# Group norms that run beside selective scans: statistics and application on ScalarE instead of VectorE

## The chip, the core and the metric

The kernel runs on one core of one Trainium2 chip. A core has a matrix engine (TensorE, PE in the profile), a vector engine (VectorE, DVE), an activation engine (ScalarE, ACT), a general engine (GpSimd, POOL) and a sync engine (SyncE, SP) that here only issues DMAs. Each engine works through its own queue in order, and the queues wait for each other through semaphores. The metric is the device time of one execution in microseconds (us), as the median of several runs.

## The reference

The input is four images of 96 channels and 64 x 64 pixels (L = 4096), in fp32. Four layers follow, each of the form x + layer(group_norm(x)):

```python
def _gn(v, G=32, eps=1e-5):          # 32 groups of 3 channels
    g = v.reshape(B_, G, C_ // G, H_, W_)
    m = jnp.mean(g, axis=(2, 3, 4), keepdims=True)
    s = jnp.var(g, axis=(2, 3, 4), keepdims=True)
    return ((g - m) / jnp.sqrt(s + eps)).reshape(v.shape)

x = x + layer0(_gn(x))    # attention to pooled positions, 5x5 depthwise convolution
x = x + layer1(_gn(x))    # four-direction selective scan, then a convolution block with a channel gate
x = x + layer2(_gn(x))    # one dense 3x3 convolution
x = x + layer3(_gn(x))    # 1x1 and depthwise convolutions, a second selective scan, a gated tail
```

A selective scan is a linear recurrence along the pixels, in four directions, for 192 channels with 16 states each: h = h * exp(delta * A) + (delta * u) * B, and y is the sum over the states of h * C.

So there are 16 group norms in all, four for each image. Each takes the mean and the variance over three channels and all pixels, subtracts the one and divides by the root of the other.

## The kernel before

**Two kinds of work side by side.** The main function is `streams`. Its scans are one long chain of *units*: eight scans (two layers times four images, in the order `SCANS`) of 384 units, 3072 units in all. A unit treats 8 channels x 16 states = 128 partitions and a chunk of 1024 pixels; twelve units make a *group* (96 channels, one chunk, one direction). All other layers are written as Python generators, `first`, `second` and `third`, one call per image, and are laid *beside* the scans by `BESIDE`: `first` of images 1, 2, 3 beside scans 0, 3, 4; `second` of the four images beside scans 1, 2, 5, 6; three `third` beside scan 7. `first(0)` runs alone ahead of the scans and `third(3)` alone after them; while they do, `solo[0]` is true.

- `first`: load x, group norm, attention (layer 0), group norm, and the input projection and depthwise convolution of layer 1 (`in_conv`).
- `second`: the rest of layer 1, group norm, the dense 3x3 convolution (layer 2), group norm, and layer 3 up to its `in_conv`, which stores the scan's input u (`u_row`, `u_col`) in DRAM.
- `third`: the rest of layer 3.

**One unit**, `unit(i)`, puts these into the engines' queues in this order: `fetch(i+4)` (SP: a DMA of 512 KB into the tile `rep`, one of ten buffers), then the first side step, `decays(i+2)` (ACT: an exponential in place on `rep`, L1815), `scan(i)` (DVE: the recurrence, L1836), `carry_on(i-1)` (ACT: one column copied, L1844), `times_c(i)` (POOL: product with C, L1848), on every third unit `collect` (PE: sum over states into `acc`), `drive(i+2)` (PE: into a PSUM tile `bx` of two buffers), perhaps a second side step, and `times_b(i+1)` (DVE: product with B, L1829). `prepare` makes the inputs of a later group in small steps, among them a logarithm (L1757), casts (L1774, L1777) and loads of u; DMAs queued by `later` go out one to three units afterwards. On every twelfth unit `output` adds `acc` to the result on DVE or copies it on ACT.

The order in each queue is this order of emission (`tc.manual_schedule()`); nothing is moved afterwards.

**How side work is portioned.** A generator yields a number for the price of the step just emitted, a tuple `(1,)` for one convolution tap, or nothing (`None`) after a matrix product, whose consumer is then emitted at the end of the unit. `Slots` runs it, on a budget that each unit tops up:

```python
owed = min(owed, 0.5) + PACE - (2.1 if i % 3 == 1 else 0.0)   # PACE = 3.5
```

Per unit there is one side step, and a second if more than 0.9 of the budget is left; in the units in which `prepare` has its first steps these take the first place. Eighteen units before the end of a scan (`LEAD` = 6), when the next scan's first group is prepared, its u must have been written. So one unit earlier, at unit 365 of 384, whatever the side work has left is emitted at once:

```python
if at == per - NG - LEAD - 1:
    work.run()
```

**The group norm before** (`group_norm`): eight `bn_stats` on slices of 512 pixels (L1043), `bn_aggr` (L1047), a product with the matrix `group` that averages over three channels (PE), a copy, a difference and a fused multiply-add on one column (DVE, L1053, L1055, L1057: the variance between the channels is added), a second product with `group`, the root on ACT (L1062), its reciprocal on DVE (L1064), and the application to four slices of 1024 pixels (DVE, L1066), in place (`xn`, the second norm's `X`) or into a padded image (`pad`). Its yields are 1, 1, 1, 1, 0.5, none, 0.5, none, 0.5, 1, 1, 1, 1.

**PSUM.** `bank()` gives one of two buffers of the tag `one` beside scans, in turn, to side work and to `prepare`; all matrix products go through the helper `mm` (L948), so that every one of them shows as this line and is told apart by its tiles.

Of the kernel before, what the change touches and what calls it, by code (L numbers as in the profile page):

```python
# [9 lines left out]
F32 = mybir.dt.float32  # L10
BF16 = mybir.dt.bfloat16
AF = mybir.ActivationFunctionType
ALU = mybir.AluOpType
AX = mybir.AxisListType
# [4 lines left out]
L = H * W  # L19
# [8 lines left out]
CH = 1024  # L28
NCH = L // CH
PCH = 512  # L30
# [162 lines left out]
def _view(t, slot, rows=None):  # L193
    n, m, shape = slot
    v = t[: rows or t.shape[0], n : n + m]
    if len(shape) == 1:
        return v
    names = "abcd"[: len(shape)]
    return v.rearrange(f"p ({' '.join(names)}) -> p {' '.join(names)}",
                       **{k: s for k, s in zip(names, shape)})  # L200
# [693 lines left out]
def streams(ctx: ExitStack, tc: tile.TileContext, x, wts, cst, out, wat, cat, flag):  # L894
# [3 lines left out]
    nc = tc.nc  # L898
    keep = ctx.enter_context(tc.tile_pool(name="keep", bufs=1))
    small = ctx.enter_context(tc.tile_pool(name="small", bufs=2))  # L900
# [17 lines left out]
    def cv(name):  # L918
        n, m, shape = cat[name]
        return _view(ct, (n if n < n0 else n - n1 + n0, m, shape))  # L920
# [11 lines left out]
    ident, group = cv("ident"), cv("group")  # L932
# [3 lines left out]
    eps, one, minus = (cols[:, j : j + 1] for j in range(3))  # L936
# [7 lines left out]
    def img(t):  # L944
        return t.rearrange("p (a b) -> p a b", b=W)

    def mm(o, lhsT, rhs, first=True, last=True):
        nc.tensor.matmul(o, lhsT=lhsT, rhs=rhs, start=first, stop=last)  # L948

    solo = [True]  # L950
    spare = []

    def bank():
        if solo[0]:
            if not spare:
                t = ps.tile([128, CH], F32, tag="bx", name="bx")
                spare.extend((t[:, PCH:], t[:, :PCH]))
            return spare.pop()
        return ps.tile([128, PCH], F32, tag="one", name="one")
# [47 lines left out]
    with tc.tile_pool(name="start", bufs=1) as T:  # L1007
# [9 lines left out]
        for tag in ("l1_", "l3_"):  # L1017
            decay[tag] = keep.tile([128, 4, E // 8], F32, name=tag + "decay")
            n, m, shape = cat[tag + "alogn"]
            src = _view(t0, (n - n2, m, shape))  # L1020
            if tag == "l3_":
                nc.scalar.activation(decay[tag], src, AF.Exp)
                src = decay[tag]
# [14 lines left out]

    def group_norm(src, dst):

        st = small.tile([96, 8, 6], F32, name="gn_st")
        for j in range(8):
            nc.vector.bn_stats(st[:, j, :], src[:, bass.ts(j, PCH)])  # L1043
            if j % 2:
                yield 1
        mv = small.tile([96, 2], F32, name="gn_mv")
        nc.vector.bn_aggr(mv, st.rearrange("p a b -> p (a b)"))  # L1047
        yield 0.5
        p1 = bank()
        mm(p1[:96, 0:1], group[:96], mv[:, 0:1])  # L1050
        yield
        g = small.tile([96, 2], F32, name="gn_g")
        nc.vector.tensor_copy(g[:, 0:1], p1[:96, 0:1])  # L1053
        d = small.tile([96, 1], F32, name="gn_d")
        nc.vector.tensor_sub(d, mv[:, 0:1], p1[:96, 0:1])  # L1055
        v = small.tile([96, 1], F32, name="gn_v")
        nc.vector.scalar_tensor_tensor(out=v, in0=d, scalar=d, in1=mv[:, 1:2], op0=ALU.mult, op1=ALU.add)  # L1057
        yield 0.5
        p2 = bank()
        mm(p2[:96, 0:1], group[:96], v)  # L1060
        yield
        nc.scalar.activation(g[:, 1:2], p2[:96, 0:1], AF.Sqrt, bias=eps[:96])  # L1062
        yield 0.5
        nc.vector.reciprocal(g[:, 1:2], g[:, 1:2])  # L1064
        for j in range(4):
            nc.vector.tensor_scalar(dst[:, 16 * j : 16 * j + 16, :], img(src)[:, 16 * j : 16 * j + 16, :],  # L1066
                                    g[:, 0:1], g[:, 1:2], ALU.subtract, ALU.mult)
            yield 1

    def diagonals(pool, w, name="diag"):  # L1070
# [229 lines left out]
    def first(b):  # L1300

        with tc.tile_pool(name="p1", bufs=1) as P:
            xn = P.tile([96, L], F32, name="xn")
            for j in range(4):
                nc.sync.dma_start(out=xn[:, bass.ts(j, CH)], in_=x[b][:, bass.ts(j, CH)])
            yield from group_norm(xn, img(xn))
            with tc.tile_pool(name="p1d", bufs=1) as D:
                samp = D.tile([96, 34, 34], F32, name="samp")
# [13 lines left out]
                with tc.tile_pool(name="p1f", bufs=1) as FP:  # L1322
                    feat = FP.tile([96, L], F32, name="feat")
                    yield from neighbours(b, xn, samp, dist, feat)
                    with tc.tile_pool(name="l0c", bufs=1) as pool:
# [12 lines left out]
                        for j in range(8):  # L1338
# [11 lines left out]
                            nc.sync.dma_start(out=res1[b][:, js], in_=xn[:, js])  # L1350
                            yield 1
            yield from group_norm(xn, img(xn))
            for j in range(4):
                nc.sync.dma_start(out=gate1[b][:, bass.ts(j, CH)], in_=xn[:, bass.ts(j, CH)])
# [20 lines left out]
    def second(b):  # L1375
# [90 lines left out]
        with tc.tile_pool(name="p2r", bufs=1) as R2:  # L1466
            hp = R2.tile([96, PADW, PADW], F32, name="hp")
            border(hp, 1)
            with tc.tile_pool(name="p2b", bufs=2) as pool:
                X = pool.tile([96, L], F32, name="X", bufs=1)  # L1470
                for j in range(4):
                    nc.sync.dma_start(out=X[:, bass.ts(j, CH)], in_=res1[b][:, bass.ts(j, CH)])
                pad = pool.tile([96, PADW, PADW], F32, name="pad2", bufs=1)
                border(pad, 1)
                w = staged(pool, "l2_k", "l3_c1", "l3_lin")
                yield from group_norm(X, pad[:, 1 : 1 + H, 1 : 1 + W])
                for j in range(8):
                    js = bass.ts(j, PCH)
                    p = bank()
                    yield from conv(p[:96], w["l2_k"], pad, j)  # L1480
                    nc.vector.tensor_add(X[:, js], X[:, js], p[:96])
                    nc.sync.dma_start(out=res2[b][:, js], in_=X[:, js])
                    yield 1

                yield from group_norm(X, img(X))
                for j in range(8):
                    js = bass.ts(j, PCH)
                    p = bank()
                    mm(p[:96], w["l3_c1"], X[:, js])
                    yield  # L1490
                    r = pool.tile([96, PCH], F32, name="r")
                    nc.scalar.activation(r, p[:96], AF.Relu, bias=bn3[1], scale=bn3[0])
                    yield 1
                    q = bank()
                    mm(q[:96], w["l3_lin"], r)
                    yield
                    nc.scalar.activation(inner(hp, j), img(q[:96]), AF.Identity, bias=wv("l3_lin_b"))
                    yield 1
# [481 lines left out]
    with tc.manual_schedule():  # L1980
# [15 lines left out]
        for i in range(total):  # L1996
            s, at = divmod(i, per)
# [29 lines left out]
    p = bank()  # L2027
# [36 lines left out]
```

## Time and profile before

| | us |
|---|---|
| median of three runs | 15068.81 (15060.3 to 15096.54) |
| the profiled execution, its own time | 15038.64 |
| its span, first to last instruction | 15036.8 |
| DVE busy | 11679.2 |
| PE busy | 12260.5 |
| POOL busy | 10375.2 |
| ACT busy | 8280.8 |
| scans on DVE, L1836 (3072, two groups) | 5401.4 + 1754.2 |
| products with B on DVE, L1829 (3072) | 3720.1 |
| products with C on POOL, L1848 (3072) | 7230.5 |
| scan factors on ACT, L1815 (3072) | 3495.9 |

The scans run from 830 us to about 14750 us of the span; each of the first seven takes 1689 to 1721 us and the eighth 1969. Busy times are unions of an engine's instructions. The mean granted clock of the matrix engine is 0.809 of full speed. A group of instructions in the profile is written as line, engine, operation, tiles written and read, shapes and count, then its busy time in us, the mean length of one in ns, and the idle time of the engine just before it, with what ended that. A line can be that of a helper. The profile's chain of work that ended last goes back only to the very end of this kernel, so stretches of time are read instead.

### The profile page before, as it was taken

The numbers are of one execution on the slowest core, as the hardware profiler recorded it, in microseconds if no ns is written. First come the engines' busy times: TensorE is split into PE (matmuls) and PEld (weight loads), VectorE is DVE, ScalarE is ACT, GpSimd is POOL, SyncE is SP. The second block draws the span as 40 slices with busy tenths as digits, with TensorE's granted clock in tenths as the row PEclk, the third lists the DMA queues.
The fourth block names the chain that finished last, engine by engine and source line by source line (L and its number), as shares of the span: only waits on it lengthen the run. The fifth ranks groups of instructions, "written<-read, shape, count | busy, mean of one in ns | idle before, by whom it ended". The sixth has DMA issues, their size and how long they took to land. (4 is left out here: it accounts for less than half of the span.)

```text
span 15036.8 us, 127166 instructions
## 1 busy us (share of the span) xinstructions
PE 12260.5 (82%) x40658; PEld 3344.2 (22%) x40658; DVE 11679.2 (78%) x7517; ACT 8280.8 (55%) x11648; POOL 10375.2 (69%) x4746
## 2 busy tenths in 40 slices
PE   8978886888969787889868887897969888667757
PEld 2322221222212222222212221221212222111111
DVE  0067888888878888778887798798878888777784
ACT  3155555555745566555655556455755567545652
POOL 0056787777868777668776787786777778666672
PEclk9978886898969888789867797797879888667666
DMA  0066788786878778667876788687877868666682
GB/s 9 26 149 163 177 202 213 175 211 171 215 178 203 195 183 209 167 168 197 208 179 158 170 204 222 174 203 180 203 195 192 203 173 221 168 166 167 167 204 68
DMA packets 902136, 2644.32 MB, mean 176 GB/s; under 512 B 107280, under 2 KB 257392, under 8 KB 901456
## 3 DMA queue, kind: packets, MB, share of 16 engines
q1 hardware_dynamic: 900800, 2634.83, 71.0%
q8 instruction: 323, 5.29, 0.2%
q14 instruction: 357, 2.92, 0.1%
q10 hardware_dynamic: 656, 1.27, 0.0%
HBM read 2169.08 MB, written 466.62 MB: 175 GB/s over the span
## 5 line engine op out<-in xcount | busy, mean ns | idle before, releaser
L1848 POOL TENSOR_TENSOR rep<-hs,bc 128x1024 f32<-128x1024 f32 x3072 | 7230.5, 2358 | 3160.0 <-DVE hs L1836 2682.5
L1836 DVE TENSOR_TENSOR_SCAN hs<-rep,carry,bx 128x1024 f32<-128x1024 f32 x2304 | 5401.4, 2344 | 277.9 <-POOL rep L1848 15.0
L1829 DVE TENSOR_TENSOR bx<-bx,bc 128x1024 f32<-128x1024 f32 x3072 | 3720.1, 1211 | 1033.6 <-PE bx L948 998.6
L1815 ACT ACTIVATE rep<-rep,l_decay 128x1024 f32<-128x1024 f32 x3072 | 3495.9, 1143 | 903.6 <-DMA rep<-dd 883.7
L948 PE MATMUL bx<-parts,spread 24*128 24x512 bf16 x6144 | 1413.5, 438 | 1812.0 <-DVE hs L1836 1762.5
L948 PE MATMUL acc<-rep,ct 128*32 128x512 f32 x12288 | 2603.0, 732 | 184.9 <-POOL rep L1848 184.9
L1836 DVE TENSOR_TENSOR_SCAN hs<-rep,bx 128x1024 f32<-128x1024 f32 x768 | 1754.2, 2284 | 306.9 <-POOL rep L1848 224.9
L948 PEld LDWEIGHTS <-spread 24*128 24x128 bf16 x6144 | 310.1, 93 | 4297.8 <-DVE hs L1836 2925.5
L948 PE MATMUL one<-band,dg 96*96 96x512 f32 x2304 | 1117.9, 621 | 0.0
L948 PE MATMUL one<-upad,diag 96*96 96x512 f32 x2016 | 1021.0, 643 | 3.2 <-ACT ur L1114 2.7
L948 PEld LDWEIGHTS acc<-rep,ct 128*32 128x32 f32 x12288 | 507.5, 126 | 1958.9 <-issue 1482.0
L948 PE MATMUL one<-qq,kk 96*128 96x512 f32 x1152 | 820.7, 802 | 133.8 <-ACT ex L1234 80.1
L1234 ACT ACTIVATE ex<-one 128x512 f32<-128x512 f32 x576 | 342.8, 595 | 754.1 <-PE one L948 749.3
L948 PE MATMUL one<-pr,ct 6*96 6x512 f32 x1024 | 647.1, 732 | 29.7 <-ACT pr L1720 4.1
L1815 ACT ACT_TABLE_LOAD x470 | 603.0, 1283 | 116.4 <-DMA rep<-dd 108.7
L948 PE MATMUL one<-hp,diag 96*96 96x512 f32 x1152 | 606.5, 665 | 48.0 <-POOL diag L1075 48.0
L948 PE MATMUL one<-vpad,diag 96*96 96x512 f32 x1200 | 590.7, 627 | 0.0
L1844 ACT COPY carry<-hs 128x1 f32<-128x1 f32 x2304 | 408.8, 177 | 314.4 <-DVE hs L1836 313.5
L948 PE MATMUL held<-ex,cols 128*32 128x256 f32 x3072 | 569.2, 451 | 12.0 <-ACT ex L1234 6.0
L948 PE MATMUL held<-ex,vT 128*32 128x256 f32 x3072 | 569.4, 451 | 0.0
L948 PEld LDWEIGHTS one<-band,dg 96*96 96x96 f32 x2304 | 350.6, 166 | 532.7 <-issue 517.1
L948 PEld LDWEIGHTS one<-upad,diag 96*96 96x96 f32 x2016 | 317.6, 172 | 490.0 <-issue 472.6
(3399 smaller groups left out, 13980.7 us busy)
## 6 DMA issues: line engine op xcount, KB each, us to landing
rep<-dd SPq DMA_DIRECT2D x3072, 512.0 KB
parts<-du SPq DMA_DIRECT2D x1024, 144.0 KB
bc<-rows SPq DMA_DIRECT2D x256, 512.0 KB
dd<-delta SPq DMA_DIRECT2D x256, 384.0 KB
du<-cut SPq DMA_DIRECT2D x256, 384.0 KB
us<-urow SPq DMA_DIRECT2D x128, 384.0 KB
du<-cut SPq DMA_DIRECT2D x256, 192.0 KB
yrow<-yo SPq DMA_DIRECT2D x128, 384.0 KB
```

The source lines that it names most:

```text
L948: nc.tensor.matmul(o, lhsT=lhsT, rhs=rhs, start=first, stop=last)
L1234: nc.scalar.activation(last.rearrange("p a b -> p (a b)"), p, AF.Exp, scale=HD**-0.5)
L1815: nc.scalar.activation(a, a, AF.Exp, scale=decay[tag][:, k, NG * h + m : NG * h + m + 1])
L1829: nc.vector.tensor_mul(bx, bx, ready[i // NG][2][:, 0, :])
L1836: nc.vector.tensor_tensor_scan(out=hs, data0=a, data1=bx, initial=carry[:, h, m : m + 1] if c else 0.0, op0=ALU.mult, op1=ALU.add)
L1844: nc.scalar.copy(carry[:, h, m : m + 1], live[i][1][:, CH - 1 : CH])
L1848: nc.gpsimd.tensor_tensor(a, hs, ready[i // NG][2][:, 1, :], ALU.mult)
```

## The change

Beside scans (`solo[0]` false) a new function takes the place of the old body; in the solo stages nothing is changed. The mean is taken from copies in place on ACT whose accumulator output gives the sum of a slice, the variance from squares of the difference on ACT (the result of the square goes into a PSUM bank that nobody reads; its accumulator output is what counts), and the application is an ACT operation with a scale and a bias per channel. DVE keeps two small reduces, the reciprocal and one product of two columns. The mean over the group is now taken before the squares, so the two passes over the image follow each other, and the new function yields 1 four times, 0.5, none, 0.5, 1 eight times, 0.5, none, 0.5, 0.5 and 1 four times.

```diff
--- before.py
+++ after.py
@@ -1038,6 +1038,9 @@
 
     def group_norm(src, dst):
 
+        if not solo[0]:
+            yield from group_norm_on_scalar(src, dst)
+            return
         st = small.tile([96, 8, 6], F32, name="gn_st")
         for j in range(8):
             nc.vector.bn_stats(st[:, j, :], src[:, bass.ts(j, PCH)])
@@ -1065,6 +1068,40 @@
         for j in range(4):
             nc.vector.tensor_scalar(dst[:, 16 * j : 16 * j + 16, :], img(src)[:, 16 * j : 16 * j + 16, :],
                                     g[:, 0:1], g[:, 1:2], ALU.subtract, ALU.mult)
+            yield 1
+
+    def group_norm_on_scalar(src, dst):
+
+        st = small.tile([96, 8], F32, name="gs_st")
+        for j in range(4):
+            s = src[:, bass.ts(j, CH)]
+            nc.scalar.activation(s, s, AF.Copy, accum_out=st[:, j : j + 1])
+            yield 1
+        mv = small.tile([96, 4], F32, name="gs_mv")
+        nc.vector.tensor_reduce(mv[:, 0:1], st[:, 0:4], AX.X, ALU.add)
+        yield 0.5
+        p = bank()
+        mm(p[:96, 0:1], group[:96], mv[:, 0:1])
+        yield
+        nc.scalar.activation(mv[:, 1:2], p[:96, 0:1], AF.Copy, scale=-1.0 / L)
+        yield 0.5
+        for j in range(8):
+            p = bank()
+            nc.scalar.activation(p[:96], src[:, bass.ts(j, PCH)], AF.Square, bias=mv[:, 1:2], accum_out=st[:, j : j + 1])
+            yield 1
+        nc.vector.tensor_reduce(mv[:, 2:3], st, AX.X, ALU.add)
+        yield 0.5
+        p = bank()
+        mm(p[:96, 0:1], group[:96], mv[:, 2:3])
+        yield
+        nc.scalar.activation(mv[:, 2:3], p[:96, 0:1], AF.Sqrt, bias=eps[:96], scale=1.0 / L)
+        yield 0.5
+        nc.vector.reciprocal(mv[:, 2:3], mv[:, 2:3])
+        nc.vector.tensor_mul(mv[:, 3:4], mv[:, 1:2], mv[:, 2:3])
+        yield 0.5
+        for j in range(4):
+            nc.scalar.activation(dst[:, 16 * j : 16 * j + 16, :], img(src)[:, 16 * j : 16 * j + 16, :], AF.Identity,
+                                 scale=mv[:, 2:3], bias=mv[:, 3:4])
             yield 1
 
     def diagonals(pool, w, name="diag"):
```

## The prediction

> **What bounds the kernel now.** I read the busy times of the page first. No engine is full over the span, so the answer has to come from stretches.
>
> ```profile
> PE 12260.5 (82%) x40658; PEld 3344.2 (22%) x40658; DVE 11679.2 (78%) x7517; ACT 8280.8 (55%) x11648; POOL 10375.2 (69%) x4746
> ```
>
> Next, the busy time of each engine in chosen stretches. Columns: stretch, length, busy us (instructions) of PE, PEld, DVE, ACT, POOL, then clock, DMA share, GB/s. The first three are group norms (seven scan units each: the second norm of `first`, both norms of `second`), the fourth has no side work (36 units), the fifth is the tail of `second`, depthwise convolutions (20 units).
>
> ```profile
> 2072.00:2106.00 34.00, 15.99 (x54) 3.50 (x54) 33.47 (x27) 15.14 (x18) 22.74 (x10) 0.60 0.86 225
> 3363.00:3399.00 36.00, 12.02 (x44) 2.79 (x44) 35.69 (x31) 10.54 (x11) 24.67 (x11) 0.57 0.78 194
> 3522.00:3558.00 36.00, 12.58 (x43) 3.04 (x44) 35.80 (x30) 12.60 (x18) 26.89 (x12) 0.53 0.79 198
> 2399.00:2540.00 141.00, 70.28 (x238) 12.41 (x236) 128.08 (x76) 71.25 (x92) 115.78 (x51) 0.58 0.88 214
> 4075.00:4157.00 82.00, 78.18 (x239) 23.09 (x238) 71.73 (x43) 63.77 (x78) 64.94 (x29) 0.92 0.80 198
> ```
>
> In a norm DVE is busy 98 to 99% and ACT a third to under half: DVE alone sets the pace, 4.9 to 5.2 us a unit. Without side work a unit takes 141/36 = 3.92 us, 3.56 of it DVE and 1.98 ACT. In the tail PE is 95% busy, 4.10 us a unit. Then the groups of DVE around a norm (3355 to 3400 us), where the third figure is idle time before the group:
>
> ```profile
> L1066 DVE TENSOR_SCALAR pad<-X,gn_g 96x1024 f32<-96x1024 f32 x4 | 5.3, 1330 | 0.0
> L1043 DVE BATCH_NORM_STATS2 gn_st<-X 96x6 f32<-96x512 f32 x8 | 5.1, 675 | 8.8 <-DMA X<-res 8.8
> L1057 DVE SCALAR_TENSOR_TENSOR gn_v<-gn_d,gn_mv 96x1 f32<-96x1 f32 x1 | 1.8, 1778 | 0.0
> ```
>
> The statistics also made DVE wait 8.8 us for the image. `gn_v` is one column wide yet takes 1.8 to 3.2 us beside scans and 0.22 in the solo stage.
>
> **What the Trainium skill says.** "SBUF — State Buffer", Who interferes with whom: DVE's two-port operations, and those with two SBUF inputs, exclude GpSimd from a shared port pair for a whole instruction; ACT waits for no one there. The trace agrees: `gn_v` above has two SBUF inputs and waits out a GpSimd product of 2.36 us. "ScalarE: Activation LUTs", What ACT_TABLE_LOAD costs: each per-partition pointer operand adds about 93 ns. The trace agrees: two pointers 776 ns (L1413), one 682 (L1434).
>
> **Removed from DVE**, per norm: 8 x 0.675 statistics = 5.4; aggregate 0.34; copy, difference and reciprocal 0.42; `gn_v` 2.5 (mean of the 14 beside scans); application 4 x 1.27 = 5.1 (mean over xn, X and pad). Sum 13.8 us, 14 norms: 193 us. The two solo norms are untouched.
>
> **Added to DVE**: two reduces of 0.15 and 0.16 (nearest rows, L1209 and L1440), reciprocal 0.14, and a product of two SBUF columns. No such product lies beside scans; bounds 0.14 (no GpSimd in the way) and 3.2 (worst `gn_v`); I take 2.5, its twin. Sum 2.95 a norm, 41 us. DVE loses 152 us net.
>
> **Added to ACT.** Prices from these rows of its groups (whole span, and for L1755 the tail):
>
> ```profile
> L1462 ACT ACTIVATE one<-V,se 96x512 f32<-96x512 f32 x32 | 21.3, 674 | 0.0
> L1434 ACT ACTIVATION_READ_ACCUMULATOR V<-one,wt 96x1 f32 x32 | 6.1, 189 | 0.0
> L1755 ACT ACTIVATE delta<-w__18893,cols 96x1024 f32<-96x1024 f32 x1 | 1.1, 1145 | 0.0
> L1062 ACT ACT_TABLE_LOAD x16 | 20.5, 1283 | 0.3
> ```
>
> Four in-place copies, 1.04 (L1774) + 0.19 = 1.23 each, 4.9. Eight squares into PSUM with a pointer, 0.67 + 0.19, 6.9. Four applications with two pointers, 1.145 + 0.09, 4.9. Two one-column operations, 0.5. Sum 17.3, of which 0.26 (the root) was there. Copy, Square and Identity have no table loads at their present lines (L1462, L1141, L1753), so the root's load and the reload after it, 2.6 us, stay as they are. ACT gains 17 x 14 = 239 us.
>
> **The planner.** A unit gives side work at most two steps, for a budget of 2.8 on average. The old norm is 11 steps, the new one 21 (a step that stops at a bare `yield` swallows the next 0.5); walked through `unit` and `Slots`, a norm takes 14 units in place of 7. So each scan with two norms needs 14 units more. In `first` the side work ends at unit 339 of 384 and would end at 353: idle units pay. In `second` it ends at unit 365 now, just where `work.run()` empties what is left (two steps). After, 35 steps are left: 31 convolution taps in one lump ahead of unit 365, in scans 1, 2, 5 and 6.
>
> **Price of the lump.** Two lines, of PE's timeline and of the waits from 4157 to 4238 us:
>
> ```profile
> 4148.92 3.67 PE L948 MATMUL one<-upad,diag 96*96 96x512 f32 x8
> PE one L948 <- DMA us<-urow: 13.9, 1, 13.9
> ```
>
> An fp32 tap leaves two records, so 62 x 0.46 = 28.5 us on PE. Behind it stand `drive(367)` on PE and `decays(367)` on ACT, the latter after the last Silu 0.68, transposing copy 1.10, table load 1.28 and exponential 1.14: 4.2. DVE meanwhile has scan 365, product 366, scan 366 and product 367, about 7.1. Stall 25.6. SP's queue stands too: the stores of u come before `fetch(369)` and before the next scan's load of u. That load already stops PE for 13.9 us here in `second` (one unit of 17.2); much of it moves into the lump: the load lands about 44 us after the lump starts and releases scan 369 at 47, where it would otherwise stand at 40; so 7 us of stall there, against 13.6 now. Net 25.6 - 6.6 = 19; I take 18 and keep 8 to 28.
>
> **The wait at the start.** The DVE waits ahead of the first statistics sum to 54 us in seven norms. Now ACT's copy waits. Behind it in ACT's queue is `decays(i+2)`, so DVE can still do two units. In-place copies also wait for the stores of res1 and res2 that read the image, which before only the application did; the last is issued a few units earlier and should have landed. I take 25 of the 54 as saved and keep 0 to 45.
>
> **The pace of a new norm.** From below DVE's own work, 3.56 + 2.95/14 = 3.77 a unit. ACT's busy time is 1.98 + (17.3 + 2.6)/14 = 3.40, so busy time alone doesn't bind. But ACT runs in order, waits 0.29 a unit for scan factors (883.7 us over 3072 units), and now has two waits per norm for a PE product, not one (5.6 us each when it waited); DVE's reduces and reciprocal wait for it. With 11 more per 14 units ACT would need 4.5. Its head start of two units hides most. I take 4.05, the no-side pace plus most of DVE's 0.21, range 3.9 to 4.2.
>
> **The sum.** The 14 norm windows last 522 us; three of them hold the pooling of `first` (5.9 each), so 504 for 98 units. The 98 further units that the new norms take displace 42 without side work (165 us) and 56 of the tail (230). Before: 899. After: 196 x 4.05 = 794, + 4 x 18 - 25 = 841. Gain 58 us of the profiled execution's 15038.6 (span 15036.8). The median shown, 15068.8, is 30 above it, with the same work; I put the gain on the median: 15010.
>
> **Rivals.** *ACT becomes the bound, slower.* If its waits add rather than hide, a norm unit takes 4.6: 902 + 72 - 0 - 899 = +75, so 15144. The point of decision is 4.22 with no start saved (4.35 with 25). For it: ACT is a single queue with 84% busy; against it: it is two units ahead and its peaks (two squares, a logarithm, two table loads) are about 4 us over three units. *The lump eats the gain.* With 30 a lump and 15 saved, 794 + 120 - 15 - 899 = 0: 15069. For it: the stall is worked out from queues, and stores follow it; against: the 13.9 us wait there overlaps. *ACT hides all.* 3.85 a unit, 10 a lump, 40 saved: 755 + 40 - 40 - 899 = -144: 14925. For it: half of ACT is idle in these windows. That the change does nothing is excluded: all norms beside scans run with `solo[0]` false.
>
> **How the numbers follow.** Likeliest 0.5 (its own range 14965 to 15055); hides all 0.2; lump eats 0.13; ACT-bound 0.17. 0.3% is 45 us, about what the three runs before (15060 to 15097) allow to tell. Faster by more: 0.38 + 0.2 + 0.02 = 0.60; slower: 0.01 + 0.04 + 0.13 = 0.18; the rest 0.22. The range 14915 to 15110 leaves out the far ends of the hiding and the ACT-bound cases, about 0.1 each.
>
> **What would show it.** Right: no batch statistics beside scans; 14 units per norm at about 4.05, DVE under 96% there and ACT about 85%; in scans 1, 2, 5, 6 one gap of 20 to 30 us in DVE near unit 366, and a smaller one at 368. Wrong: DVE idle until ACT in the norms (ACT bound); the squares or copies dearer than 0.86 and 1.23 us; copies waiting for stores; a gap near 366 under 10 or over 35; table loads more by dozens.

## The result, and the profile after

| | before | after |
|---|---|---|
| median of the runs, us | 15064.56 (4 runs, 15033.04 to 15096.54) | 14969.51 (4 runs, 14956.75 to 14979.04) |
| ratio to before | | 0.9936, 95% interval 0.9922 to 0.9950 |
| span of the profiled execution, us | 15036.8 | 14977.2 |
| DVE busy, us | 11679.2 | 11520.2 |
| ACT busy, us | 8280.8 | 8460.1 |

The kernel became 0.64% faster, 95 us by the medians. The two profiled executions differ by less, 60 us: that of before was among the fastest of its kernel and that of after was the slowest of its own. The direction and the range of the prediction held; its gain, 58 us, was short of the medians' 95 and close to the profiles' 60, the latter in part by luck, as the sum at the end shows.

The busy times on the page of after: VectorE lost 159 us (152 were worked out), ScalarE gained 179 (239 were worked out). Busy time counts once what successive instructions of an engine overlap, about 0.1 us in these records; the durations themselves, added up, fell by 178 us on VectorE and rose by 219 on ScalarE, which also has twelve fewer table loads (15 us) at the Silu of the convolutions.

```profile
PE 12331.1 (82%) x40658; PEld 3357.0 (22%) x40658; DVE 11520.2 (77%) x7335; ACT 8460.1 (56%) x12041; POOL 10361.2 (69%) x4746
```

The busy times in stretches of after, in the same columns as before (PE, PEld, DVE, ACT, POOL, clock, DMA share, GB/s). The first three are the same three norms, now 14 units each; the last has the final 20 units ahead of unit 365 in scan 1 and the start of what follows.

```profile
2071.00:2125.00 54.00, 27.35 (x96) 5.96 (x90) 49.32 (x34) 42.34 (x57) 44.32 (x20) 0.63 0.89 229
3319.00:3373.00 54.00, 31.39 (x97) 7.49 (x100) 50.67 (x34) 42.27 (x61) 43.84 (x20) 0.60 0.86 220
3484.00:3537.00 53.00, 28.24 (x107) 6.49 (x104) 49.02 (x33) 43.83 (x74) 46.25 (x21) 0.66 0.88 225
4008.00:4092.00 84.00, 76.45 (x210) 21.15 (x210) 67.93 (x41) 60.72 (x82) 61.73 (x27) 0.84 0.78 202
```

A unit of a norm takes 54/14 = 3.86 us at most, where it took 4.9 to 5.2; DVE is at 91 to 94%, ACT at 78 to 83%. Counted from unit 180 on, with the wait for the image, the fourteen units of the first norm of `second` take 58 to 60 us in the four scans; before, these units took 76 to 82. This is not yet a gain, since before seven of them also held steps of the convolution behind the norm, which now come later.

The new groups on DVE, over the whole span:

```profile
L1100 DVE TENSOR_TENSOR gs_mv<-gs_mv 96x1 f32<-96x1 f32 x14 | 10.7, 766 | 0.5
L1099 DVE RECIPROCAL gs_mv<-gs_mv 96x1 f32<-96x1 f32 x14 | 2.1, 151 | 8.5 <-ACT gs_mv L1097 8.5
L1092 DVE TENSOR_REDUCE gs_mv<-gs_st 96x1 f32<-96x8 f32 x14 | 2.0, 145 | 9.2 <-ACT one L1090 9.2
L1081 DVE TENSOR_REDUCE gs_mv<-gs_st 96x1 f32<-96x4 f32 x14 | 2.0, 144 | 19.3 <-ACT xn L1078 12.3 <-ACT X L1078 7.0
```

All waits of DVE for ACT in these lines together are 37 us in 14 norms, 2.6 each; another 18 us are waits for `decays` at the start of five norms. So ScalarE did not become the bound. What the change cost stands at the end of the four scans beside `second`. The timeline of DVE there (scan 1, start and length in us, idle time and its end in brackets), three lines of PE's and three of SP's:

```profile
4124.42 1.23 DVE L1866 TENSOR_TENSOR bx<-bx,bc 128x1024 f32<-128x1024 f32 x1 [20.38 <-PE bx L948]
4128.43 2.35 DVE L1873 TENSOR_TENSOR_SCAN hs<-rep,carry,bx 128x1024 f32<-128x1024 f32 x1 [2.77 <-ACT rep L1852]
...
4148.58 1.23 DVE L1866 TENSOR_TENSOR bx<-bx,bc 128x1024 f32<-128x1024 f32 x1 [14.20 <-PE bx L948]
```

```profile
4109.73 14.33 PE L948 MATMUL one<-upad,diag 96*96 96x512 f32 x33
4123.99 0.60 PE L948 MATMUL bx<-parts,spread 24*128 24x512 bf16 x4
4141.84 3.64 PE L948 MATMUL one<-us,wt 96*38 96x512 f32 x8 [17.25 <-DMA us<-urow]
```

```profile
4109.35 15.76 SPq L1153 DMA_DIRECT2D urow<-ur  x3
4125.91 3.45 SPq L1156 DMA_DIRECT2D ucol<-uc  x4
...
4132.83 2.96 SPq L1735 DMA_DIRECT2D us<-urow  x2
```

This is the lump. PE is in convolution taps until 4124, DVE waits 20.4 us for `drive` and 2.8 more for `decays`; the stores of u leave SP's queue only as the lump ends, so the next scan's load of u goes out at 4132.8, lands at 4141.8, and DVE waits another 14.2 us. Scan to scan the two gaps are 26.7 us (3.6 would be undisturbed) and 17.9 us; in the other three such scans 26.7 and 17.2 to 18.1.

Counted by scans of the two profiles, the three beside `first` are 28, 23 and 24 us shorter and the four beside `second` 4, 8, 1 and 10 us longer: beside `second` the lump takes back what the norms gave. In scan 1 after is 22 us ahead at unit 352, with 31 taps still to do, and 4 us behind at unit 368.

### The profile page after: what moved, and what is told of

Same layout as the page of the kernel before. It is cut to its first block, busy times and chain, and to the rows that moved or that the text cites. A ratio compares the mean times of both kernels' runs of the same rounds, so it can differ in the third digit from the quotient of the medians.

```text
span 14977.2 us, 127407 instructions
## 1 busy us (share of the span) xinstructions
PE 12331.1 (82%) x40658; PEld 3357.0 (22%) x40658; DVE 11520.2 (77%) x7335; ACT 8460.1 (56%) x12041; POOL 10361.2 (69%) x4746
## 4 chain that ended last, share of the span: by engine, by line
PE 47%; DVE 19%; ACT 9%; DMA 7%; POOL 7%; issue 6%; SPq 1%; DVEq 0%; POOLq 0%; ACTq 0%
PE one L948 30%; DVE hs L1873 13%; PE acc L948 8%; PE bx L948 7%; DVE bx L1866 5%; DMA rep<-dd 4%; POOL rep L1885 4%; PE held L948 2%; ACT rep L1852 2%; ACT L1852 1%; POOL V L1408 1%; DMA yc<-ycol 1%; ACT ex L1271 1%; POOL delta L1797 0%; ACT delta L1792 0%
## 5 line engine op out<-in xcount | busy, mean ns | idle before, releaser
L948 PE MATMUL acc<-rep,ct 128*32 128x512 f32 x12288 | 2676.8, 751 | 178.7 <-POOL rep L1885 177.8
L948 PE MATMUL one<-upad,diag 96*96 96x512 f32 x2016 | 990.4, 631 | 0.0
```

## The experiments

Each ratio is against runs of the kernel before on the same chip, and kernels from different chips are compared by their ratios. Where two ratios are subtracted, their intervals leave an uncertainty of some 30 us. Theory: every microsecond taken from VectorE in a norm is gained, and the planner's part, the lump, is a loss of its own. Rivals: ScalarE's new queue is a limit; the convolution taps cost the same wherever they stand; the gain is in how many units a norm takes.

**The planner's part alone.** All work of the norm stays on VectorE, and ten empty steps are put in, so that it has 21 steps as after (below: the spread norm).

```diff
         yield 0.5
+        if not solo[0]:
+            for _ in range(8):
+                yield 1
+            yield 0.5
         p2 = bank()
...
         nc.vector.reciprocal(g[:, 1:2], g[:, 1:2])
+        if not solo[0]:
+            yield 0.5
```

> The kernel before, all of the norm's work still on VectorE, but with ten empty side steps put into each norm beside scans, so that it has the 21 steps of the changed one and side work slips as there. Theory (the planner's part of the change is a pure loss of one lump, about 25 us in each of four scans, and spreading VectorE's 13.8 us over 14 units gains nothing since VectorE is full in either case): about 90 to 110 us slower than before, about 15160. Rival (taking 14 units instead of 7 is itself what gains, since idle units are cheap): within 30 us of before or faster.

Measured: 15122.59 us, ratio 1.0039 (1.0024 to 1.0053), 58 us slower than before. At equal steps the move to ScalarE is thus worth 1.0039 - 0.9936 = 1.03%, 155 us give or take 30, against 152 us of DVE time worked out. The planner's part is a loss, but of about half the size expected. The starts of the units' recurrences in the traces tell where. As sums over the four scans beside `second`, in us against the kernel before:

| units of the scan | after | the spread norm |
|---|---|---|
| 180 to 240, both norms | -174 | -84 |
| 240 to 364, the tail | +108 | +102 |
| 364 to the end, with the lump | +86 | +91 |

So beside `second` both halves of the theory hold in these executions: what spreading gains in the norms comes back in the tail, to which the displaced steps move, and the lumps are left; the four scans are 99 us longer. The three scans beside `first` are 7 us shorter, 8 longer and 22 shorter, and the last scan, in which nothing was changed, is 10 shorter. Stretches that no run changed differ by up to 24 us between single executions (units 0 to 180 of scan 2 take 802 to 826 us in the eleven kernels that are alike there), so why 58 us were measured and not 100 stays open. The stretch of a norm in this kernel (14 units):

```profile
3353.00:3415.00 62.00, 26.52 (x86) 5.78 (x87) 60.62 (x48) 25.37 (x29) 47.10 (x20) 0.53 0.74 184
```

62/14 = 4.4 us a unit, with DVE full. With the wait for the image these fourteen units take 70 to 71 us in the four scans, between the 76 to 82 of before and the 58 to 60 of after.

**The lump alone.** The changed kernel with more budget, only in the scans beside `second` and only behind both norms.

```diff
-            owed = min(owed, 0.5) + PACE - (2.1 if i % 3 == 1 else 0.0)
+            owed = min(owed, 0.5) + PACE + (0.3 if s in (1, 2, 5, 6) and at >= 240 else 0.0) - (2.1 if i % 3 == 1 else 0.0)
```

> The changed kernel with the budget raised to 3.8 in scans 1, 2, 5 and 6 from unit 240 on, that is only after both norms: nothing in front of it moves, the side work ends at unit 364, nothing is left for the lump, and the load of u stops PE as before. It asks for the lump alone. Theory (a lump stalls VectorE where spread taps do not): the unit of 26.7 us becomes about 4 and the four scans gain 15 to 23 us each: 60 to 90 us faster than the changed kernel, about 14890. Rival (PE is 95 percent busy in the tail, so the 28 us of taps lengthen the units they are spread over by as much): within 20 us of the changed kernel, about 14960.

Measured: 14840.03 us, ratio 0.9850 (0.9836 to 0.9865), 0.86% or 130 us (give or take 30) less than the change alone, more than the 60 to 90 expected. The DVE timeline at the same place, where both the product and the scan that had waited now follow at once:

```profile
4113.10 2.35 DVE L1873 TENSOR_TENSOR_SCAN hs<-rep,carry,bx 128x1024 f32<-128x1024 f32 x1
4115.36 1.21 DVE L1866 TENSOR_TENSOR bx<-bx,bc 128x1024 f32<-128x1024 f32 x1
4116.70 2.35 DVE L1873 TENSOR_TENSOR_SCAN hs<-rep,carry,bx 128x1024 f32<-128x1024 f32 x1
...
4132.05 1.23 DVE L1866 TENSOR_TENSOR bx<-bx,bc 128x1024 f32<-128x1024 f32 x1 [9.40 <-PE bx L948]
```

The gap of 26.7 us is 3.6, and the second one fell from about 17.7 to 13. By the profiles the four scans are 20, 47, 38 and 20 us shorter, 125 together, and 111 of these lie behind unit 364, some 28 in each scan, where the lump and the load stood.

The taps that had stood in the lump cost no time in their new places: the tail, units 240 to 364, takes 540 to 543 us with them, where it took 542 to 549 without. These are the lines of that stretch of scan 1, first of the changed kernel and then of this one:

```profile
3549.20:4094.50 545.30, 493.19 (x1422) 135.10 (x1422) 443.16 (x263) 378.64 (x489) 412.60 (x186) 0.86 0.76 192
3562.50:4105.90 543.40, 489.32 (x1487) 138.81 (x1490) 443.70 (x263) 389.14 (x499) 412.77 (x186) 0.92 0.77 195
```

With the taps of the lump PE has 65 matmul records more here, in slightly less busy time, since the clock granted to it was higher: in the four tails 0.86 to 0.87 of full speed in the changed kernel, 0.91 to 0.92 here. The traces record this clock as either full or half; a record of a tap lasts 592 ns in the median at the full clock and 1061 at half. So the rival, that PE must pay for the taps anyway, is not refuted; it paid, and the clock gave it back. Why the clock is higher with the larger budget was not tried, and the theory did not speak of it. What the run shows is that the ends of the scans lost their stall.

**The same from the start of the scan.** 3.55 in place of 3.5 in these scans, for after and for before.

```diff
-            owed = min(owed, 0.5) + PACE - (2.1 if i % 3 == 1 else 0.0)
+            owed = min(owed, 0.5) + PACE + (0.05 if s in (1, 2, 5, 6) else 0.0) - (2.1 if i % 3 == 1 else 0.0)
```

> The changed kernel with the budget of a unit raised from 3.5 to 3.55 in scans 1, 2, 5 and 6 alone. Walked through the planner, the side work of those scans then ends at unit 357 and nothing is left for unit 365. Theory (the lump of 31 taps is a stall of its own, about 23 us in each of four scans, and the load of u behind it stops PE for 13 us where it need only stop it for 5): the gap of 26.7 us at unit 366 is gone and the one of 17 to 18 us at unit 368 falls to about 8; 4 x (23 + 9) = 128 us less than the changed kernel, less some 30 us because the taps now fill other units: 80 to 130 us faster than it, about 14860. Rival (PE has to do the taps anyway, and PE is 95 percent busy where they go): within 30 us of the changed kernel, about 14950.

> The kernel before with the same raised budget in scans 1, 2, 5 and 6: what the budget is worth without the change of the norms. It has no lump now (two steps are left), so theory: only the load of u gains, 4 x 9 = 36 us faster than before, about 15030. Rival (a larger budget packs all side work better and is the gain by itself): 80 us or more faster than before.

Measured: on the changed kernel 14929.56 us, ratio 0.9916 (0.9903 to 0.9928), 30 us less than after by the ratios, no more than the uncertainty, far from the theory and at the edge of the rival. Its gaps at the end are gone (3.6, and 7.0 to 9.2 at the load), but on the kernel before the same budget costs 0.1%: 1.0010 (1.0003 to 1.0016), where 36 us of gain were forecast. In both the earlier layers of `second` are dearer: scan 1 of the kernel before with this budget is 11 us behind at unit 160 and 34 at 176, before its norms. Both forecasts missed: I had priced only the end. The late budget avoids this.

**The late budget where there is no lump.** The budget of 3.8 from unit 240 on the kernel before, and on the spread norm of VectorE.

> The kernel before with the budget raised to 3.8 from unit 240 on in scans 1, 2, 5 and 6 (side work then ends at unit 353). What the late budget is worth with no lump to remove. Theory (its gain of 130 us over the changed kernel is the lump, 4 x 23 to 27, and the load of u, 4 x 5 to 9): here only the load, 20 to 40 us faster than before, about 15025. Rival (the late budget gains by packing the last layers better): 80 us or more faster than before.

> The norm on VectorE with 21 steps (slow_steps) and the late budget of 3.8: no lump. Theory (of slow_steps' 58 us over before, the lump makes more than all): about 110 us faster than slow_steps and about 50 us faster than before, near 15005; against the changed kernel with the same late budget (14840) it then lacks VectorE's 152 us. Rival (the lump is worth less where VectorE is the limit): within 40 us of slow_steps.

Measured: 15094.05 us, 1.0018 (1.0012 to 1.0025), and 15018.20 us, 0.9966 (0.9953 to 0.9978). Without a lump the budget alone makes the kernel slower, not 20 to 40 us faster. The part that was forecast came: behind unit 364 the four scans are 38 us shorter. But their tails, units 240 to 364, are 15 to 21 us longer each, 73 together, which the forecast had left out. In the tail of scan 1 (3560 to 4100 us) DVE waits longer for `bx`, which PE has behind the taps, 44.1 us:

```profile
DVE bx L1829 <- PE bx L948: 44.1, 30, 9.1
```

The same line has 32.0 us in 15 waits in the kernel before. The clock granted to PE in these tails is also lower, 0.88 to 0.89 where it was 0.90 to 0.91.

With the spread norm the budget gives 0.73%, 110 us by the ratios (104 by the medians), as expected. By the profiles its four scans are 111 us shorter behind unit 364, the same as on the changed kernel, and as long as before in the tail (4 us more together), where the granted clock is 0.91 to 0.92 and was 0.86 to 0.89. So in both kernels with a lump the gain is what stood at the end of the scans, the lump with the load behind it, as the theory says, and not a better packing, which would show in the tails. That the taps are free in the tail hangs on the clock. With the late budget on both sides the move to ScalarE is worth 0.9966 - 0.9850 = 1.16%, 175 us.

**More of it.** The changed kernel with 3.95.

> The changed kernel with the late budget at 3.95: side work ends at unit 358 instead of 364, so the stores of u are out of the sync queue before the load. Theory: the unit of 13 us at 368 falls to about 8, 4 x 5 = 20 us faster than at 3.8, about 14820. Rival (PE has no room left in the tail): the same as at 3.8 or slower, 14840 to 14870.

Measured: 14888.54 us, 0.9880 (0.9866 to 0.9894), slower than 3.8 by 0.3%, as the rival said and by more than its 30 us. The waits of DVE in the tail of scan 1 (3533 to 4090 us), first with 3.8 and then with 3.95:

```profile
DVE bx L1866 <- PE bx L948: 35.3, 23, 10.4
```

```profile
DVE bx L1866 <- PE bx L948: 47.7, 32, 11.1
```

In the four scans units 240 to 364 take 554 to 555 us, where 3.8 has 540 to 543: 49 us more together, against 16 saved behind unit 364.

**The application alone, both ways.** Only the application to ScalarE, on the kernel before (11 steps kept); and back to VectorE, on the changed kernel.

```diff
+            nb = small.tile([96, 1], F32, name="gn_b")
+            nc.vector.scalar_tensor_tensor(out=nb, in0=g[:, 0:1], scalar=-1.0, in1=g[:, 1:2], op0=ALU.mult, op1=ALU.mult)
...
+                nc.scalar.activation(dst[:, 16 * j : 16 * j + 16, :], img(src)[:, 16 * j : 16 * j + 16, :], AF.Identity,
+                                     scale=g[:, 1:2], bias=nb)
```

```diff
-            nc.scalar.activation(dst[:, 16 * j : 16 * j + 16, :], img(src)[:, 16 * j : 16 * j + 16, :], AF.Identity,
-                                 scale=mv[:, 2:3], bias=mv[:, 3:4])
+            nc.vector.tensor_scalar(dst[:, 16 * j : 16 * j + 16, :], img(src)[:, 16 * j : 16 * j + 16, :],
+                                    mv[:, 2:3], mv[:, 3:4], ALU.mult, ALU.add)
```

> The kernel before with the application alone moved to ScalarE; the statistics stay on VectorE, and the steps are those of before (11), so the planner's part is the same. VectorE loses 5.1 us a norm and gains one product of 0.8. Theory (VectorE's saved time is the gain, one for one): 14 x 4.3 = 60 us faster than before, about 15000. Rival (the gain comes from the statistics, where VectorE waits for the image, and the application hides anyway): within 20 us of before.

> The changed kernel with the application back on VectorE; statistics on ScalarE, 21 steps, the same lump. Theory (VectorE's time counts one for one): 14 x 5.1 = 71 us slower than the changed kernel, about 15035, some 25 us faster than before. Rival (in four units near the end of a norm VectorE can take 1.3 us each without loss, since it is not full there): within 20 us of the changed kernel.

Measured: 14973.30 us, 0.9945 (0.9932 to 0.9958), 83 us or 5.9 a norm against 4.3 expected (the added product took 0.16 us in all 14 norms, not 0.8, so that 4.9 would have been due); and 15014.63 us, 0.9971 (0.9960 to 0.9981), 0.35% or 53 us slower than after, 3.8 a norm against 5.1. VectorE's busy time fell by 67 us in the first run and rose by 65 in the second, so it counts about one for one in both places; whether it counts for more where VectorE is full and for less where the norm is spread, these intervals can't tell. The application alone, with no slip of the planner, is as fast as the whole change within the intervals (0.9945 beside 0.9936): the lump took about as much as the statistics gave.

**ScalarE as the limit.** Two copies, squares or applications in a step, 13 steps in place of 21, so that ScalarE's load is packed into 8 to 10 units and no lump is left.

```diff
             nc.scalar.activation(s, s, AF.Copy, accum_out=st[:, j : j + 1])
-            yield 1
+            if j % 2:
+                yield 1
```

(the same under the squares and the applications)

> The changed kernel with two copies, two squares and two applications in a step: 13 steps and 8 to 9 units a norm, two steps left at unit 365, so no lump. ScalarE's load in a norm unit rises from 3.0 to about 4.2 us, over VectorE's 3.6. Theory (ScalarE's head start of two units can't hide a load above VectorE's for 8 units): norm units of 4.2 to 4.6 us, bound by ScalarE; against the changed kernel the four scans with a lump gain 25 us each and the norms lose about 5 us each: 20 to 50 us faster than the changed kernel, about 14930. Rival (the head start hides it): norm units stay at 3.85 and it is 80 to 110 us faster than the changed kernel, about 14870.

Measured: 14897.41 us, 0.9894 (0.9882 to 0.9907), 63 us less than after by the ratios, between the two. A norm in it lasts ten units, 41.3 us, so 4.1 a unit:

```profile
3493.00:3534.00 41.00, 21.62 (x78) 4.78 (x75) 35.00 (x25) 32.83 (x58) 33.73 (x16) 0.60 0.87 223
```

and one of its units has DVE waiting for the last square (DVE's timeline):

```profile
3509.93 1.21 DVE L1869 TENSOR_TENSOR bx<-bx,bc 128x1024 f32<-128x1024 f32 x1
3515.14 0.16 DVE L1094 TENSOR_REDUCE gs_mv<-gs_st 96x1 f32<-96x8 f32 x1 [4.00 <-ACT one L1091]
```

Both engines are at 80 to 85% here and neither alone is full. Most units stay at 3.6 us and one goes to 7.5: the head start is spent at one point, the reduce. So a wait for ScalarE does appear at this density, though ScalarE is not full; at 21 steps it stays small.

> The kernel with two operations a step (pairs) and the budget raised to 3.6 in scans 1, 2, 5 and 6 from unit 240 on: the side work ends at unit 360, so the stores of u have left the sync queue before the next scan's load. Theory (that load stops PE 9 us less in each of the four scans): about 35 us faster than pairs, about 14860. Rival (the earlier taps cost as much as the load gains): within 15 us of pairs, about 14900.

```diff
-            owed = min(owed, 0.5) + PACE - (2.1 if i % 3 == 1 else 0.0)
+            owed = min(owed, 0.5) + PACE + (0.1 if s in (1, 2, 5, 6) and at >= 240 else 0.0) - (2.1 if i % 3 == 1 else 0.0)
```

Measured: 14846.68 us, 0.9859 (0.9843 to 0.9875), 0.35% or 53 us less than without the budget, against 35 expected. It is as fast as the 21 steps with the late budget (0.9850, whose interval overlaps). Either is 1.4 to 1.5% faster than the kernel before and about 0.8% faster than the changed one.

## Why the prediction was right or wrong

**What bounds a norm: right.** DVE was full there, and its time was the gain: 155 us measured at equal steps (the changed kernel against the spread norm), give or take 30, where DVE's busy time fell by 159. That the 152 worked out stand so near is in part luck: the product was priced 24 us too dear, and the overlap of successive instructions, some 18 us, was not taken off.

**Removed and added on DVE: one price wrong.** The product of two columns (L1100) takes 0.77 us on average, from 0.16 to 1.32, not 2.5. Its twin `gn_v` was the wrong stand-in: how long such an instruction stands depends on what GpSimd is in the midst of, and the product comes at another point of the unit. It made 24 us: 152 + 24 = 176, and the durations on DVE fell by 178.

**Added on ACT: right.** The durations rose by 219 us, which with the twelve table loads that fell away makes 234 of the 239. Copy 1.04 + 0.19, square 0.68 + 0.19, application 1.23, root 0.26, each within 2% of its price; no table load was added at the new lines, and the in-place copies of second norms waited for no store (the first copy had no idle time ahead of it in all seven).

**The pace of a new norm: too dear.** I took 4.05 us; the eleven norms without the pooling of `first` take 3.84 on average (14 units each). The term that was mis-sized is the pace without side work, on which the 4.05 was built: its 3.92 held stalls, among them one unit of 7.4 us at the load of u and one of 6.6. Without a stall a unit is 3.6 us, and 4.5 with an output, every twelfth, so 3.68 on average; DVE's new work and its waits for ACT added 0.16 to that. 196 x 0.21 = 41 us more gain. This is the case of the rival "ACT hides all", whose 3.85 it is.

**The wait at the start: right in kind, smaller.** Ahead of the first norm of `second` DVE idled 8.8 us; it now waits 3.4 for `decays` behind ACT's copy and 1.8 for the reduce:

```profile
DVE hs L1873 <- ACT rep L1852: 3.4, 1, 3.4
DVE gs_mv L1081 <- ACT X L1078: 1.8, 1, 1.8
```

Over the seven norms the waits at the start fell from 54 to 38 us: some 16 us were saved, not 25.

**The lump: right in place and size, wrong in what it overlaps.** The gap is 23.1 us longer than an undisturbed unit; 25.6 were worked out. The 6.6 us that I took off, because the load's stall would lie inside, were not there. The load did land where I put it, 45 us after the lump began, but behind it PE still has a projection of 3.64 us and a collection of 2.8 before `drive`; these I had left out. So the load's gap stayed at 17.2 to 18.1. Net 23, not 18: 20 us less gain.

**The sum.** The forecast of 58, with 41 more for the pace, 9 less for the start and 20 less for the lump, gives 70 us, against 60 between the two profiles and 95 between the medians. So the forecast came close to the profiles in part by luck: its errors, of 41 and of 29 us, have opposite signs. What is left can't be assigned, since unchanged stretches differ by up to 24 us between single executions. One thing was neither priced nor tried: in the tails of after PE was granted a clock of 0.86 to 0.87, where before it was 0.90 to 0.91.

**The rivals.** ACT-bound: excluded at 21 steps (2.6 us of waits in the norm's own lines, 4.0 with those for `decays` at the start, and a pace of 3.84); at 13 steps single waits of 4 us appear. The lump eats the gain: true beside `second`, where four scans together are 23 us longer, not for the kernel. ACT hides all: right on the pace, wrong on the lump.

## What to carry to other kernels

A move of work between engines has two prices: the engines' time, and what its new number of steps does to a schedule by budget. Here the second took back 0.86 of 1.5 percent, because the old budget ended exactly where a deadline empties the rest in one block; find such a deadline before a change, and set the budget again after it. A block of 31 taps in front of the scans cost 23 us of stall, since every queue stopped behind it, and the load behind it kept its full wait; spread over the units before, the same taps cost no time here, where the granted clock was higher, but the kernel before lost time by a denser tail. So try such a budget on each kernel, and look at the whole scan and not only at its end.

## What the runs showed of the hardware

A VectorE instruction on one column with two operands in SBUF took 0.22 us alone, 1.8 to 3.2 in one place beside GpSimd's products (`gn_v`) and 0.16 to 1.32 in another (L1100): its time is set by where it stands against GpSimd, not by its size. In 25 of these 28 norms it ended 12 to 19 ns after the end of a GpSimd instruction, and the other three took 0.16 us. In seven of the fourteen cases of `gn_v` it stood through a second GpSimd instruction, which had started later than itself, as here in the kernel before (two lines of POOL's timeline and one of DVE's):

```profile
3537.05 2.33 POOL L1764 TENSOR_TENSOR t__16130<-delta,us 96x1024 f32<-96x1024 f32 x1
3539.34 2.33 POOL L1848 TENSOR_TENSOR rep<-hs,bc 128x1024 f32<-128x1024 f32 x1
3538.56 3.13 DVE L1057 SCALAR_TENSOR_TENSOR gn_v<-gn_d,gn_mv 96x1 f32<-96x1 f32 x1
```

An accumulating ACT copy in place takes 1.04 us for 96 x 1024, as long as the copies of that size without an accumulator (1.03 to 1.05 us, with a cast), and 0.19 more for reading the sum. Where no wait stood in the way, units ran at 3.6 us to within 0.1 over whole stretches, in kernels with quite different side work: the recurrence and the product on DVE (2.35 + 1.21) set that. The clock granted to PE in the tail of scan 1 was 0.86 with one budget of the side work and 0.92 with another, and the record of a tap lasted 592 ns at the full clock and 1061 at half; what moved the clock is not shown.
